# Cross-attention on one core: x's rows copied by ScalarE into two banks of PSUM, onto which the output's products are added, in place of GpSimd's additions

## The chip, the cores and the metric

The kernel runs on one core of a Trainium2 chip. The metric is the time of the program in microseconds of the device; the median of two runs of the kernel before is 1415.7 us (1415.37 and 1416.03). The engines are named as in the profile: PE is TensorE (matmuls), PEld its loading of weights, DVE is VectorE, ACT is ScalarE, POOL is GpSimd, SP is SyncE, which here issues nearly all transfers.

## The reference

For each of 64 images, x has 256 rows of 512 and the context 256 rows of 384, all in float32:

```python
text_p = einsum('bld,dh->blh', H_l, W_text) + b_text
audio_p = einsum('bsd,dh->bsh', H_a, W_audio) + b_audio
Q = layer_norm(text_p, g1, beta1)
K = layer_norm(audio_p, g2, beta2)
V = audio_p
scores = einsum('blh,bsh->bls', Q, K) * scale
alpha = softmax(scores)
H_hyper = einsum('bls,bsh->blh', alpha, V)
H_hyper = einsum('blh,hk->blk', H_hyper, W_out) + b_out
return layer_norm(H_hyper + H_l, g_out, beta_out)
```

H_l is x, and the last line adds x to the output's product before the last normalisation. That addition is what the change moves.

## The kernel before, in words

W_audio and W_out are folded once into one matrix wao of 384x512 with a bias bao (fold_multiply L248, fold_bias L263), so that an image's output is softmax times context, times wao, plus bao, plus x.

**Tiles.** An image is 256 rows, two tiles of 128 partitions. Each of the three large products of an image (q, k and y, class Blocks, L466) is made of seven products of blocks instead of eight: L487 multiplies sums of blocks of the left side by sums of blocks of the weights, and leave() (L491 to L515) adds the seven results into the quarters of the output with VectorE. GpSimd makes the sums of the left sides: sum_x (L310, xsum), sum_c (L326, csum for k, zsum for y). The seven results stand in four banks of PSUM, in pairs: (1,6), (2,5), (3,4) and (7). A bank holds 128x512 float32. leave(1) puts product 1 plus the bias into the upper half of the output's rows; leave(6), leave(2,5), leave(3,4) and leave(7) each add to what stands there, so they follow one another. Every bank read by leave is an addition of 128x512 on VectorE at L499.

**Banks.** PSUM has eight banks here. The pool p_pj (L81) has six, used in turn: a request takes the bank that was asked for six requests earlier and waits until that one's last reader is done. The pool p_at (L82) has two, for the scores (L526), the context products (ps_z, L592) and transposes.

**Order.** The schedule is written by hand: each engine carries out its instructions in the order in which the program names them, and waits on semaphores for what it needs of others. The main loop (L886) works on several images in one pass. With b as the pass: scores and softmax of image b (at); the q and k products of image b+2; the context and the y products of image b-1 (last); the rest of the output of image b-2 (done). A pass's order, as far as the change touches it:

- at.scores(), then done.o.leave(3,4), done.o.leave(7) and done.add_x(): the last two banks of y leave and GpSimd adds x's rows to y's rows (L608, two instructions of 128x512)
- turn_next: VectorE's transposes (L91) of x and the context of a later image, GpSimd's xsum and csum
- maxima and exponentials, q's first two products and leaves, division of e
- done.statistics(): ScalarE reads y's rows for mean and squares (L617, L622)
- q's other products and leaves, q's squares on ScalarE (L392) and their roots on GpSimd (L353, L355)
- q.turn (L91), done.shift (L729), last.context (the z products L592, zT copied by ScalarE L599), q.affine and k.affine (ScalarE L458), k.turn (L451), done.settle (L738), done.store
- q's normalise (ScalarE L420) and store
- last.start_products(): GpSimd makes zsum (L331 to L334)
- k's seven products and leaves, k's squares (L392), roots, normalise (L420) and store
- y's products: (1,6), their leaves, (2,5), their leave, (3,4), (7); the leaves of (3,4) and (7) fall in the next pass

Images 62 and 63 are worked off behind the loop with plain matmuls (L639, L692) and add x in another way (L648, L772), which the change leaves alone.

x's rows (x_rows) are loaded in a pass (L112, 512 KB) and, until now, first read two passes later, by add_x. The pool xin has three buffers.

Of the kernel before, what the change touches and what calls it, by code (L numbers as in the profile page):

```python
# [9 lines left out]
F32 = mybir.dt.float32  # L10
AF = mybir.ActivationFunctionType
ALU = mybir.AluOpType
AX = mybir.AxisListType
PSUM = bass.MemoryType.PSUM

P = 128
# [6 lines left out]
def kernel(  # L23
# [41 lines left out]
    nc = tc.nc  # L65
    ctx.enter_context(tc.manual_schedule())
    B, L, D = x.shape
    S, DA = c.shape[1:]
    H = w_text.shape[1]
    LT, ST = L // P, S // P  # L70
# [7 lines left out]
    work = ctx.enter_context(tc.tile_pool(name="work", bufs=2))  # L78
    small = ctx.enter_context(tc.tile_pool(name="small", bufs=4))
    scratch = ctx.enter_context(tc.tile_pool(name="scratch", bufs=3, space=bass.MemoryType.DRAM))  # L80
    p_pj = ctx.enter_context(tc.tile_pool(name="p_pj", bufs=6, space=PSUM))  # L81
    p_at = ctx.enter_context(tc.tile_pool(name="p_at", bufs=2, space=PSUM))  # L82

    def squares(dst, src):
# [11 lines left out]
    def load_c(b):  # L96
        cq = blk.tile([P, S // SQ, DA // NQ], F32, tag="cq", name=f"cq_{b}")
        squares(cq, c[b])
        blocks[b] = [cq]

    def load_x(b):
        xq = blk.tile([P, L // SQ, D // NQ], F32, tag="xq", name=f"xq_{b}")
        squares(xq, x[b])
        blocks[b].append(xq)
# [5 lines left out]
    def load_x_rows(b):  # L110
        x_rows[b] = xin.tile([P, LT, D], F32, tag="x", name=f"x_{b}")
        nc.sync.dma_start(x_rows[b], x[b].rearrange("(t p) d -> p t d", p=P))  # L112

    def load_c_rows(b):
        c_rows[b] = cin.tile([P, ST, DA], F32, tag="c", name=f"c_{b}")
        nc.sync.dma_start(c_rows[b], c[b].rearrange("(t p) d -> p t d", p=P))
# [16 lines left out]
    def row(v, name):  # L133
        t = const.tile([P, H], F32, tag=name, name=name)
        nc.sync.dma_start(t, v.rearrange("(o h) -> o h", o=1).broadcast_to([P, H]))
        return t
# [8 lines left out]
    x_rows, c_rows = {0: x_0}, {0: c_0}  # L145
# [54 lines left out]
    class RowTurn:  # L200


        def __init__(self, rows_sb, chunks, name):
            self.rows, self.chunks = rows_sb, chunks
            tag = "yr" if chunks == DC else "kT"
            self.ar = work.tile([P, 2, chunks, P], F32, tag=tag, name=f"{name}r")
            self.T = work.tile([P, chunks, 2 * P], F32, tag=name, name=f"{name}_0")
# [38 lines left out]
    ps_wao = {}  # L246

    def fold_multiply(a):  # L248

        ps = ps_wao[a] = p_pj.tile([P, D], F32, tag="pj", name="ps_wao")  # L250
        for k in range(HC):
            nc.tensor.matmul(  # L252
                ps,
                lhsT=waT[k][:, bass.ts(a, P)],
                rhs=wo_sb[:, k, :],
                start=(k == 0),
                stop=(k == HC - 1),
            )
# [32 lines left out]
    H2 = H // 2  # L291
# [34 lines left out]
    def sum_c(cT, tag="csum"):  # L326

        part = lambda i, j: cT[:, j, bass.ts(i, P)]
        s = work.tile([P, 5, P], F32, tag=tag, name=tag)
        add = nc.gpsimd.tensor_tensor  # L330
        add(s[:, 0], part(1, 0), part(1, 1), ALU.add)  # L331
        add(s[:, 1], s[:, 0], part(0, 0), ALU.subtract)
        add(s[:, 2:4], cT[:, 0:3:2, :P], cT[:, 0:3:2, P:], ALU.subtract)
        add(s[:, 4], part(0, 1), s[:, 1], ALU.subtract)  # L334
        return {
            1: [part(0, 0)], 2: [part(0, 1), part(0, 2)], 4: [part(1, 1), part(1, 2)],
            5: [s[:, 0], part(1, 2)], 6: [s[:, 1]], 7: [s[:, 2]], 3: [s[:, 4], s[:, 3]],
        }
# [127 lines left out]
    class Blocks(Projection):  # L466
# [7 lines left out]
        def __init__(self, name, b, sides, weights, bias):  # L474
            super().__init__(name, b, None, None, bias, None, 2)
            self.sides, self.weights, self.banks = sides, weights, {}

        def products(self, *ns):

            for n in ns:  # L480
                group = next(g for g in ((1, 6), (2, 5), (3, 4), (7,)) if n in g)
                if group not in self.banks:
                    self.banks[group] = p_pj.tile([P, 2, H2], F32, tag="pj", name=f"ps_{self.name}")
                place = self.banks[group][:, group.index(n), :]
                pairs = list(zip(self.sides[n], self.weights[n]))
                for i, (side, w) in enumerate(pairs):
                    nc.tensor.matmul(  # L487
                        place, lhsT=side, rhs=w, start=(i == 0), stop=(i == len(pairs) - 1)
                    )

        def leave(self, *ns):  # L491
# [22 lines left out]
    class Attention:  # L514
# [86 lines left out]
        def start_products(self):  # L601

            self.o = Blocks("y", self.b, sum_c(self.zT, "zsum"), wao_blocks, bao_sb)
            self.y = self.o.rows

        def add_x(self):
            for t in range(LT):
                nc.gpsimd.tensor_tensor(self.y[:, t, :], self.y[:, t, :], x_rows[self.b][:, t, :], ALU.add)  # L608

        def statistics(self, lo=0, n=LT):  # L610

# [151 lines left out]
    def turn_next(b):  # L763
        xT[b] = turn_x(b)
        xs[b] = sum_x(xT.pop(b))
        cT[b] = turn_c(b)
        cs[b] = sum_c(cT.pop(b))

    def add_bias(b):
        xb = x_rows[b]  # L770
        for t in range(LT):
            nc.gpsimd.tensor_tensor(xb[:, t, :], xb[:, t, :], bao_sb, ALU.add)  # L772

    assert B > 3
    q, k, xT, cT = {}, {}, {}, {}
# [66 lines left out]
    xs = {1: sum_x(xT[1])}  # L842
    k[1].scales()
    fold_multiply(0)
    fold_multiply(1)
    g1_sb, be1_sb, g2_sb, be2_sb, bac_sb = take_columns()

# [27 lines left out]
    cT[2] = turn_c(2)  # L875
    cs[2] = sum_c(cT[2])
    fold_multiply(2)
    fold_evict(2)
    bao_sb = fold_bias(part)
# [5 lines left out]
    done = last = None  # L885
    for b in range(B - 2):  # L886
        three = b + 3 < B
        at = Attention(b)
        at.scores()
        if done:  # L890
            done.o.leave(3, 4)
            done.o.leave(7)
            done.add_x()
        if three and b:
            turn_next(b + 3)
        if last:
            last.turn_e()
        at.maxima()
        at.exponentials()
        if not b:  # L900
            k[1].turn()
        q2 = q[b + 2] = Blocks("q", b + 2, xs.pop(b + 2), wt_blocks, bt_sb)
        q2.products(*((1, 6) if b else (1, 2, 6)))
        q2.leave(1)
        q2.leave(6)
        at.reciprocals()
        at.divide_e()
        if not b:
            k[1].affine(g2_sb, be2_sb)
        if b:  # L910
            q[b + 1].fetch()
            k[b + 1].fetch()
        at.store_e()
        if b + 4 < B:
            load_c(b + 4)
        if not b:
            at.fetch_e()
        if b + 4 < B:
            load_x(b + 4)
        if b:  # L920
            at.fetch_e()
            load_x_rows(b)
            load_c_rows(b)
        if not three:
            load_x_rows(b + 1)
            load_c_rows(b + 1)
        if b == 1:
            go_sb = row(g_out, "go")
            beo_sb = row(beta_out, "beo")
        if done:  # L930
            done.statistics()
        q2.products(*((2, 5) if b else (5,)))
        q2.leave(2, 5)
        q2.products(3, 4)
        q2.leave(3, 4)
        q2.products(7)
        q2.leave(7)
        q2.square()
        q2.scales()
        q[b + 1].turn()  # L940
        if not b:
            turn_next(3)
        if done:
            done.shift(0)
            done.shift(1)
        if last:
            last.context()
        q[b + 1].affine(g1_sb, be1_sb)
        if b:
            k[b + 1].turn()  # L950
            k[b + 1].affine(g2_sb, be2_sb)
        if done:
            done.settle(0)
            done.settle(1)
            done.store()
        q2.normalise()
        q2.store()
        if last:
            last.start_products()
        k2 = k[b + 2] = Blocks("k", b + 2, cs.pop(b + 2), wa_blocks, ba_sb)  # L960
        k2.products(1, 6)
        k2.leave(1)
        k2.leave(6)
        k2.products(2, 5)
        k2.leave(2, 5)
        k2.products(3, 4)
        k2.leave(3, 4)
        k2.products(7)
        k2.leave(7)
        k2.square()  # L970
        k2.scales()
        k2.normalise()
        k2.store()
        if last:
            last.o.products(1, 6)
            last.o.leave(1)
            last.o.leave(6)
            last.o.products(2, 5)
            last.o.leave(2, 5)
            last.o.products(3, 4)  # L980
            last.o.products(7)
        done, last = last, at
# [7 lines left out]
    at.scores(end=True)  # L990
    done.o.leave(3, 4)
    done.o.leave(7)
    done.add_x()
    add_bias(B - 2)
    last.turn_e()
    at.maxima()
# [19 lines left out]
    last.o.products(7, 3)  # L1016
    last.o.leave(3, 4)
    last.o.leave(7)
    last.add_x()
    at.context()  # L1020
    done.settle(1)
    done.store()
# [72 lines left out]
```

## Time and profile before

| what | value |
|---|---|
| median of two runs | 1415.7 us (1415.37 to 1416.03) |
| span of the profiled execution, first to last instruction | 1411.8 us |
| span below the median | 3.9 us |
| mean granted TensorE clock | 0.999 of full speed |
| main loop, one pass | 21.58 us |
| TensorE busy in one pass (721.44 to 743.02 us) | 21.58 us |
| VectorE, ScalarE, GpSimd busy in that pass | 19.09, 14.58, 13.52 us |
| DMA's share in that pass | 0.85 |

The profile gives for the profiled execution its span alone; the time of a run also holds what lies around the span.

The rows that belong to the change are GpSimd's additions of x at L608 (124 of 1277 ns, 155.7 us in all) and the groups of L499. A group's line gives line, engine, operation, tiles and shape, count, busy time, mean of one in ns, and then the engine's idle time just before these instructions and what ended most of it. An engine's idle time costs nothing by itself where the engine is not the one that sets the pace. TensorE's rows: a float32 matmul shows as two rows, and a row of 128x256 reads 379 ns although a new row begins every 0.216 us, since they overlap.

### The profile page before, as it was taken

How to read it: one execution, taken by the hardware profiler on the slowest of the kernel's cores; microseconds unless marked ns; L12 is line 12 of the kernel's file. 1: busy time of each engine (PE TensorE's matmuls, PEld its weight loads, DVE VectorE, ACT ScalarE, POOL GpSimd, SP SyncE). 2: the span in 40 equal slices, each digit the busy share in tenths (PEclk: the TensorE clock that was granted, in tenths of full speed). 3: DMA queues.
4: the chain of work that ended last, by engine and by line, in shares of the span. 5: the costliest groups of instructions: out<-in, count | busy, mean ns of one | idle time of the engine just before them, and what ended most of it. 6: DMA issues, size and time to landing. Idle time of an engine off the chain costs nothing.

```text
span 1411.8 us, 22761 instructions
## 1 busy us (share of the span) xinstructions
PE 1403.2 (99%) x6437; PEld 1220.4 (86%) x6437; DVE 1230.4 (87%) x1758; ACT 935.0 (66%) x2298; POOL 871.0 (62%) x1294
## 2 busy tenths in 40 slices
PE   9999999999999999999999999999999999999998
PEld 5888888888888888888888888888888888888885
DVE  6888898898888988988988889889889888898887
ACT  4667667676676676676766766766767667667663
POOL 5556666656656666666566566666665665666645
PEclk9999999999999999999999999999999999999999
DMA  8798877888888887787887887877888888878763
GB/s 211 206 259 229 245 233 218 246 232 224 241 243 219 232 233 228 234 226 237 231 230 235 225 238 232 231 232 232 221 243 237 222 240 239 222 235 232 223 212 125
DMA packets 450437, 322.32 MB, mean 228 GB/s; under 512 B 154885, under 2 KB 382981, under 8 KB 450310
## 3 DMA queue, kind: packets, MB, share of 16 engines
q1 hardware_dynamic: 450214, 320.72, 80.3%
q8 instruction: 52, 0.85, 0.3%
q14 instruction: 75, 0.61, 0.2%
q10 hardware_dynamic: 96, 0.13, 0.0%
HBM read 203.83 MB, written 116.92 MB: 227 GB/s over the span
## 4 chain that ended last, share of the span: by engine, by line
PE 98%; DVE 1%; POOL 1%; DMA 0%; ACT 0%; issue 0%; DVEq 0%; ACTq 0%
PE ps_q L487 27%; PE ps_k L487 21%; PE ps_y L487 20%; PE ps_sc L526 15%; PE ps_z L592 12%; PE ps_wao L252 1%; PE ps_y L639 1%; PE ps_q L374 0%; PE ps_k L374 0%; DMA c<-in_ctx_dram 0%; DVE yr L499 0%; PE ps_rows L214 0%; POOL yr L608 0%; POOL x L772 0%; DVE kr L499 0%; PE ps_wa L227 0%
## 5 line engine op out<-in xcount | busy, mean ns | idle before, releaser
L499 DVE TENSOR_TENSOR qr<-ps_q,qr 128x512 f32<-128x512 f32 x252 | 174.3, 692 | 88.9 <-PE ps_q L487 86.1
L526 PE MATMUL ps_sc<-kT,qT 128*128 128x256 f32 x1024 | 231.5, 379 | 0.0
L353 POOL TENSOR_SCALAR ve<-var 128x2 f32<-128x2 f32 x126 | 43.4, 344 | 290.0 <-ACT junk L392 289.8
L526 PEld LDWEIGHTS ps_sc<-kT,qT 128*128 128x128 f32 x1024 | 194.6, 190 | 26.9 <-issue 0.5
L543 ACT ACTIVATE e<-ps_sc,nmx 128x256 f32<-128x256 f32 x128 | 59.4, 468 | 230.3 <-DVE nmx L536 230.3
L608 POOL TENSOR_TENSOR yr<-yr,x 128x512 f32<-128x512 f32 x124 | 155.7, 1277 | 70.8 <-DVE yr L499 70.8
L499 DVE TENSOR_TENSOR kr<-ps_k,kr 128x512 f32<-128x512 f32 x252 | 174.4, 692 | 22.5 <-DVE kr L499 0.9
L487 PE MATMUL ps_q<-wtsum,xsum 128*128 128x256 f32 x756 | 193.7, 379 | 0.0
L499 DVE TENSOR_TENSOR yr<-ps_y,yr 128x512 f32<-128x512 f32 x248 | 171.6, 692 | 21.7 <-DVE yr L499 0.5
L487 PE MATMUL ps_k<-wa,cT 128*128 128x256 f32 x630 | 177.1, 379 | 0.0
L592 PE MATMUL ps_z<-eT,c 128*128 128x256 f32 x768 | 176.2, 379 | 0.0
L487 PE MATMUL ps_y<-wao,zT 128*128 128x256 f32 x620 | 174.1, 379 | 0.0
L355 POOL TENSOR_TENSOR rstd<-ve,nhalf 128x2 f32<-128x2 f32 x192 | 157.3, 819 | 16.0
L592 PEld LDWEIGHTS ps_z<-eT,c 128*128 128x128 f32 x768 | 145.9, 190 | 20.3 <-issue 0.5
L487 PEld LDWEIGHTS ps_q<-wtsum,xsum 128*128 128x128 f32 x756 | 143.6, 190 | 19.5
L458 ACT ACTIVATE qT<-qT,columns 128x256 f32<-128x256 f32 x256 | 133.0, 593 | 4.1 <-DVE qT L91 4.0
L458 ACT ACTIVATE kT<-kT,columns 128x256 f32<-128x256 f32 x256 | 132.2, 588 | 2.3 <-DVE kT L91 1.3
L487 PEld LDWEIGHTS ps_k<-wa,cT 128*128 128x128 f32 x630 | 119.6, 190 | 16.2
L487 PEld LDWEIGHTS ps_y<-wao,zT 128*128 128x128 f32 x620 | 117.7, 190 | 16.0
L420 ACT ACTIVATE kr<-kr,rstd 128x512 f32<-128x512 f32 x126 | 84.0, 714 | 71.6 <-POOL rstd L355 71.6
L392 ACT ACTIVATE junk<-kr 128x512 f32<-128x512 f32 x126 | 79.4, 630 | 77.9 <-DVE kr L499 73.5
L487 PE MATMUL ps_q<-wt,xT 128*128 128x256 f32 x504 | 129.0, 379 | 0.0
(160 smaller groups left out, 2976.3 us busy)
## 6 DMA issues: line engine op xcount, KB each, us to landing
kd<-kr SPq DMA_DIRECT2D x64, 512.0 KB, 3.1
kq<-kd SPq DMA_DIRECT2D x256, 128.0 KB, 3.4
qd<-qr SPq DMA_DIRECT2D x64, 512.0 KB, 4.8
qq<-qd SPq DMA_DIRECT2D x256, 128.0 KB, 3.3
xq<-in_x_dram SPq DMA_DIRECT2D x252, 128.0 KB, 3.0
x<-in_x_dram SPq DMA_DIRECT2D x63, 512.0 KB, 4.3
out_dram<-yr SPq DMA_DIRECT2D x62, 512.0 KB, 4.8
cq<-in_ctx_dram SPq DMA_DIRECT2D x252, 96.0 KB, 2.5
```

Source lines behind the costliest of these rows:

```text
L252: nc.tensor.matmul(ps, lhsT=waT[k][:, bass.ts(a, P)], rhs=wo_sb[:, k, :], start=(k == 0), stop=(k == HC - 1),)
L353: nc.gpsimd.tensor_scalar(ve, var, EPS, None, ALU.add)
L355: nc.gpsimd.tensor_tensor(r, ve, nhalf[:, :n], ALU.pow)
L392: nc.scalar.activation(junk, self.rows[:, t, :], AF.Square, scale=1.0 / math.sqrt(H), accum_out=self.var[:, t : t + 1],)
L420: nc.scalar.mul(row, row, self.r[t])
L458: nc.scalar.activation(self.T[:, k, :], self.T[:, k, :], AF.Identity, bias=bet[:, k : k + 1], scale=gam[:, k : k + 1],)
L487: nc.tensor.matmul(place, lhsT=side, rhs=w, start=(i == 0), stop=(i == len(pairs) - 1))
L499: add = lambda o, i0, i1: nc.vector.tensor_tensor(o, i0, i1, ALU.add)
L526: nc.tensor.matmul(self.sc[:, t, :], lhsT=self.qT[:, k, bass.ts(t, P)], rhs=self.kT[:, k, :], start=(k == 0), stop=(k == HC - 1),)
L543: nc.scalar.activation(self.e[:, t, :], self.sc[:, t, :], AF.Exp, bias=self.nmx[:, t : t + 1], accum_out=self.den[:, t : t + 1],)
L592: nc.tensor.matmul(ps[:, j, :], lhsT=c_rows[self.b][:, s, bass.ts(lo + j, P)], rhs=self.eT[:, s, :], start=(s == 0), stop=(s == ST - 1),)
L608: nc.gpsimd.tensor_tensor(self.y[:, t, :], self.y[:, t, :], x_rows[self.b][:, t, :], ALU.add)
```

## The change

p_pj gets four banks instead of six, and a new pool p_sd gets the other two. y's blocks are seeded: in start_products, behind zsum, GpSimd subtracts one quarter of x's rows from another in place (128x256), and ScalarE copies two pairs of quarters (128x512 each) into the two banks of p_sd. The products (2,5) and (3,4) of y are then added onto these banks: their first matmul has start=False. The two matmul groups that make the first two parts of wao use the same two banks at the head. add_x and its three calls go. The in-place subtraction makes up for leave(3,4), which builds the first quarter of the output from the third, where x's third quarter then already is. The order of all other instructions on every engine stays: TensorE, VectorE and SyncE have the same instructions in the same order, ScalarE has 124 copies more, GpSimd 124 additions less and 62 subtractions more.

```diff
-    p_pj = ctx.enter_context(tc.tile_pool(name="p_pj", bufs=6, space=PSUM))
+    p_pj = ctx.enter_context(tc.tile_pool(name="p_pj", bufs=4, space=PSUM))
+    p_sd = ctx.enter_context(tc.tile_pool(name="p_sd", bufs=2, space=PSUM))
...
     def fold_multiply(a):
-        ps = ps_wao[a] = p_pj.tile([P, D], F32, tag="pj", name="ps_wao")
+        pool, tag = (p_sd, "sd") if a < 2 else (p_pj, "pj")
+        ps = ps_wao[a] = pool.tile([P, D], F32, tag=tag, name="ps_wao")
...
             self.sides, self.weights, self.banks = sides, weights, {}
+            self.seeded = ()
+
+        def seed(self, rows):
+
+            self.seeded = ((2, 5), (3, 4))
+            quarters = rows.rearrange("p t (k h) -> p (t k) h", k=2)
+            nc.gpsimd.tensor_tensor(quarters[:, 0], quarters[:, 0], quarters[:, 2], ALU.subtract)
+            for group, some in zip(self.seeded, (quarters[:, 1:3], quarters[:, 0:4:3])):
+                self.banks[group] = p_sd.tile([P, 2, H2], F32, tag="sd", name="ps_sd")
+                nc.scalar.copy(self.banks[group], some)
...
                     nc.tensor.matmul(
-                        place, lhsT=side, rhs=w, start=(i == 0), stop=(i == len(pairs) - 1)
+                        place,
+                        lhsT=side,
+                        rhs=w,
+                        start=(i == 0 and group not in self.seeded),
+                        stop=(i == len(pairs) - 1),
+                        skip_group_check=group in self.seeded,
                     )
...
             self.o = Blocks("y", self.b, sum_c(self.zT, "zsum"), wao_blocks, bao_sb)
+            self.o.seed(x_rows[self.b])
             self.y = self.o.rows
-
-        def add_x(self):
-            for t in range(LT):
-                nc.gpsimd.tensor_tensor(self.y[:, t, :], self.y[:, t, :], x_rows[self.b][:, t, :], ALU.add)
...
             done.o.leave(7)
-            done.add_x()
```

The same call of add_x goes at two places behind the loop.

More of the change, by code (lines that the diff above doesn't have):

```diff
@@ L992 @@
     done.o.leave(7)
-    done.add_x()
     add_bias(B - 2)
@@ L1018 @@
     last.o.leave(7)
-    last.add_x()
     at.context()
```

## The prediction

> **What bounds the kernel now.** I read the page first, for the engine without idle time; then the chain that ended last, to see whether the same engine carries it; then the timeline of one steady pass of the main loop, engine by engine, since the change moves work between engines that the average calls free.
>
> ```profile
> span 1411.8 us, 22761 instructions
> PE 1403.2 (99%) x6437; PEld 1220.4 (86%) x6437; DVE 1230.4 (87%) x1758; ACT 935.0 (66%) x2298; POOL 871.0 (62%) x1294
> PE 98%; DVE 1%; POOL 1%; DMA 0%; ACT 0%; issue 0%; DVEq 0%; ACTq 0%
> ```
>
> TensorE is busy for 99% of the span and makes 98% of the chain. The lists of waits put nothing in front of a matmul but a few tenths of a microsecond at the head and the tail. So GpSimd's 62% and ScalarE's 66% are no limit by themselves: no work taken from them can shorten the loop. Only a new wait in front of TensorE can change the time much, and the search is for one.
>
> VectorE, TensorE, ScalarE and GpSimd in the same pass (columns: start us, us from first to last, engine, line, tiles, idle before and its releaser):
>
> ```profile
> 714.30 0.69 DVE L499 TENSOR_TENSOR qr<-ps_q,qr 128x512 f32<-128x512 f32 x1 [0.17 <-PE ps_q L487]
> 714.91 1.23 DVE L91 STREAM_TRANSPOSE qT<-qq 128x1024 f32<-128x1024 f32 x1
> 716.07 1.37 DVE L729 SCALAR_TENSOR_TENSOR yr<-yr,nm,go 128x512 f32<-128x512 f32 x2
> 717.36 1.29 DVE L451 STREAM_TRANSPOSE kT<-kq 128x512 f32<-128x512 f32 x2
> 718.58 2.07 DVE L738 SCALAR_TENSOR_TENSOR yr<-yr,rstd,beo 128x512 f32<-128x512 f32 x2
> 720.57 0.68 DVE L499 TENSOR_TENSOR kr<-ps_k,ba 128x512 f32<-128x512 f32 x1
> 721.28 3.08 DVE L499 TENSOR_TENSOR kr<-ps_k,kr 128x512 f32<-128x512 f32 x4
> ```
> ```profile
> 721.00 0.59 PE L487 MATMUL ps_k<-wasum,csum 128*128 128x256 f32 x2
> 721.44 0.59 PE L487 MATMUL ps_y<-wao,zT 128*128 128x256 f32 x2
> 722.30 1.03 PE L487 MATMUL ps_y<-wao,zT 128*128 128x256 f32 x4
> ```
> ```profile
> 716.18 0.56 ACT L599 COPY zT<-ps_z 128x512 f32<-128x512 f32 x1
> 721.11 1.32 ACT L420 ACTIVATE qr<-qr,rstd 128x512 f32<-128x512 f32 x2
> 723.60 0.63 ACT L392 ACTIVATE junk<-kr 128x512 f32<-128x512 f32 x1 [1.17 <-DVE kr L499]
> ```
> ```profile
> 718.92 1.17 POOL L333 TENSOR_TENSOR zsum<-zT 128x256 f32<-128x256 f32 x1
> 720.05 0.91 POOL L334 TENSOR_TENSOR zsum<-zT,zsum 128x128 f32<-128x128 f32 x1
> 727.36 2.50 POOL L608 TENSOR_TENSOR yr<-yr,x 128x512 f32<-128x512 f32 x2 [1.15 <-DVE yr L499]
> ```
>
> The reader is to see a lag. TensorE has finished k's products and starts y's at 721.44 (a matmul is two rows, one row every 0.2159 us; a pass is 100 rows, 21.585 us). VectorE at that moment has only just begun to take k's banks out: leave(1) at 720.57, leave(6) from 721.28 to 721.97 (0.69 for one), then (2,5), (3,4), (7) every 0.80 us. It was held from 714.30 by the last q bank, which only TensorE's own order releases, and ran from there without idle time. TensorE does not notice, since six banks let it run ahead.
>
> **The change, part by part.** *Removed:* 124 additions on GpSimd, 1277 ns each (155.7 us on the page), two per pass. They lie beside TensorE's scores, and xsum, which follows them, is wanted a pass later. Worth nothing to the loop.
>
> *Six banks become four.* Each pass asked the pool p_pj for 12 banks in turn: q's four, k's four, y's four. Request n takes the bank of request n-6, so y's (1,6) took q's (3,4), which VectorE had left at 714.13. Now a pass asks for 10 (y's (2,5) and (3,4) come from p_sd) and request n takes the bank of n-4: y's (1,6) takes k's (1,6). The order of instructions in the changed kernel shows the same: the first matmul of y waits for VectorE's leave(6) of this pass's k. That ends at 721.974 and TensorE wants the bank at 721.437: 0.537 late. Set beside the times of this trace, every other bank that the loop asks for is free in time. This one is late by 0.53 to 0.54 us in each of 58 passes, and by 1.27, 1.37 and 0.15 in the first three.
>
> *What a wait costs beyond its lateness.* One such wait stands in the trace, at the tail:
>
> ```profile
> 1382.09 0.45 POOL L332 TENSOR_TENSOR zsum<-zsum,zT 128x128 f32<-128x128 f32 x1
> 1382.59 0.73 PEld L487 LDWEIGHTS ps_y<-waosum,zsum 128*128 128x128 f32 x4 [0.51 <-POOL zsum L332]
> ```
>
> GpSimd ends at 1382.54, the weight load starts at 1382.59, and the second matmul row stands 0.32 behind the first in place of 0.216: 0.05 + 0.11 = 0.16 us. So the wait is 0.537 + 0.16 = 0.70 us per pass.
>
> *Does it come back each pass?* Yes: VectorE's next q bank waits for TensorE, so a later TensorE moves the whole stretch 714.30 to 721.97. The loop is then y, scores and q on TensorE (66 rows, 14.25 us, and 0.20 to VectorE's start), 7.67 us on VectorE from the last q bank to the end of k's leave(6), and 0.16: 22.28 us against 21.585, again 0.70.
>
> *Added on ScalarE:* two copies of 128x512 per pass behind the normalising of q, which ends at 722.43 (instructions overlap by 0.09, so the first copy starts at 722.34). Nearest rows: the copy out of PSUM, 0.56, and the slowest 128x512 row on this engine that carries no bias, 0.71. I take 0.57, since it is the same operation. The first copy ends at 722.91; with 0.16 y's (2,5) can start at 723.07. Behind the late (1,6) products it would want to start at 721.974 + 0.16 + 4 x 0.216 = 723.00. So the seed adds 0.07 (0.21 at 0.71; 0 if the copy takes under 0.50). The second copy has 1.7 us more. Behind the copies stand the squares of k, which today wait 1.17 us until 723.60; both copies end by then, at 723.4 to 723.7. The copies' own waits are for x's rows (loaded a pass earlier) and for banks that VectorE left some 16 us before.
>
> *Added on GpSimd:* one subtraction 128x256 behind zsum, 0.73 (xsum's row) to 1.17 (L333 beside VectorE). It ends by 722.1 and is wanted by the second copy, at 722.9: hidden. If that slack were gone, y's (3,4) still has until 724.6.
>
> *SyncE's queue* is unchanged, instruction for instruction, and so is the number of matmuls; a matmul that adds to its bank shows the same 379 ns row as one that does not.
>
> *Head and tail.* At the head the third product of W_out takes the bank of q's (1,6) of image 1: wanted at 38.57, left at 40.90, so 2.33 + 0.16 = 2.5 us once. The first three passes then add 0 (VectorE's backlog there is worked off behind the same delay) to 2.4; I take 1. At the tail the additions were in front of zsum, where TensorE lost some 0.1 us: nothing.
>
> **Sum:** 58 x 0.77 + 2.5 + 1 = 48 us on a span of 1411.8. The span is 3.9 below the median 1415.7, which I take as lying around it both times: 1415.7 + 48 = 1464.
>
> **Two gates, nearly tied.** Without any lateness of leave(6), y's (2,5) would start at 722.30, as now; the first copy lets it start at 723.07 at the earliest. ScalarE alone therefore costs 0.77 us per pass: its work from the division of e at 711.50 to 722.43 runs without a pause of note, and it too starts behind a q bank that only TensorE frees. The two waits overlap, and are not to be added up: the later one counts, 0.77.
>
> [...] The settling rows of VectorE (L738, median 1104 ns in the loop, 744 on the last image's rows) are slow beside zsum, not beside the removed additions, while a leave beside those additions keeps its 692. By the rows the instruction that slows VectorE stays, and nothing is won. [...] For the copy the row out of PSUM is 0.56. [...]
>
> **Rivals.** (1) *The lag is used up once, no real change.* TensorE waits at the first y, and from there on runs later against VectorE and ScalarE, which keep their places and finish in time. Price: 0.77 + 3.5, 1420. It decides if neither engine waits for TensorE's q: VectorE's idle time there would have to be nothing. For it: the 1.27, 1.37 and 0.15 of the first passes, where VectorE works off a backlog. Against it: in the pass shown VectorE idles 0.32, 0.24, 1.04 and 0.17 us for q's banks, 1.77 in all, so it follows TensorE. (2) *ScalarE becomes the bound alone.* A write to PSUM is not in the trace. If it went at the pace of the SBUF row L458 (593 ns for 256 columns, so 1.18 for 512), y's (2,5) would start at 723.68 and not 722.30: 1.38 per pass, 80 + 3.5, 1499. Against it: the copies of 512 out of PSUM at 0.56 to 0.57. (3) *The subtraction meets VectorE.* At 1.17 in place of 0.73 beside k's leaves it could push them by up to 0.2 each pass, 0.90 in all: 52 + 3.5, 1471. Against it: the 692 of a leave beside L608. (4) *VectorE's stretch gets shorter.* If settling ran at 0.745, 2.07 would become 1.41 and leave(6) would be in time; the copy would hold the 0.77, and the time stays 1464. It is no way back by itself.
>
> **How the numbers follow.** Forecast, with (4): 0.80; rival (1) 0.06; (2) 0.07; (3) 0.06; something faster 0.01. Low end: the lateness alone, 58 x 0.537 = 31, 1446. High end: 58 x (0.70 + 0.21 + 0.2) + 5 = 69, 1485. The measurement tells about 2%, 28 us, from no change: slower than 1444 is the forecast with (2) and (3), 0.92 with a hundredth left out for a partial wait; within 2%, 0.07.
>
> **What would show it.** Right: TensorE idle about 0.75 us once per pass in front of ps_y<-wao,zT, most of it released by VectorE's kr at leave(6), the rest by ScalarE's first copy, busy share near 96%, a pass of about 22.35 us; VectorE's idle time in front of q's banks grown by the same; ScalarE's copies near 0.57. Wrong: no idle time there (rival 1), or idle time of over 1 us in front of the (2,5) products released by ScalarE (2), or settling or k's leaves longer than now (3).

## The result, and the profile after

The changed kernel takes 1472.15 us (median of two runs, 1471.81 to 1472.5) against 1415.7: a ratio of 1.040, with a 95% interval of 1.038 to 1.042. It is slower by 56.5 us. The profiled execution has a span of 1470.0 us against 1411.8, 58.2 more. In every run that lists both, the time lies 1.7 to 1.9 us above the span (1471.81 above 1470.0 here), so the span of 1411.8 belongs to an execution of about 1413.6 us, 2 us quicker than the median; that is why the spans differ by more than the medians.

The page of the changed kernel, its first lines and the engines' shares of the chain:

```profile
span 1470.0 us, 22586 instructions
PE 1422.3 (97%) x6437; PEld 1211.5 (82%) x6437; DVE 1230.6 (84%) x1758; ACT 996.7 (68%) x2422; POOL 761.6 (52%) x1232
PE 46%; DVE 29%; DMA 11%; issue 7%; ACT 4%; SPq 3%; POOL 0%; DVEq 0%; ACTq 0%
```

GpSimd has lost 109 us of work and ScalarE has gained 62, as the change intends. Yet the span grew. TensorE carries out the same 6437 rows, but where it made 98% of the chain it now makes 46%: the chain leaves TensorE wherever TensorE waits. It passes through VectorE, and from there on to ScalarE and to transfers. The transfers do not set the pace: between 80 and 1430 us the lists of waits of TensorE, VectorE, ScalarE and GpSimd name no transfer.

A steady pass of the changed kernel, each engine around the start of y (columns as in the prediction):

```profile
727.25 0.68 DVE L516 TENSOR_TENSOR kr<-ps_k,ba 128x512 f32<-128x512 f32 x1
727.96 3.08 DVE L516 TENSOR_TENSOR kr<-ps_k,kr 128x512 f32<-128x512 f32 x4
728.77 0.30 PEld L499 LDWEIGHTS ps_y<-wao,zT 128*128 128x128 f32 x2 [0.89 <-ACT qr L422]
728.80 0.67 PE L499 MATMUL ps_y<-wao,zT 128*128 128x256 f32 x2 [0.52 <-DVE kr L516]
729.02 1.09 ACT L488 COPY ps_sd<-x 128x512 f32<-128x512 f32 x2
729.64 0.73 PEld L499 LDWEIGHTS ps_sd<-wao,zT 128*128 128x128 f32 x4
729.74 1.04 PE L499 MATMUL ps_sd<-wao,zT 128*128 128x256 f32 x4
730.28 0.63 ACT L394 ACTIVATE junk<-kr 128x512 f32<-128x512 f32 x1 [0.17 <-DVE kr L516]
```

leave(6) is the first of the four rows from 727.96 and ends at 728.66. The weight load of y's first matmul starts 0.11 us later. ScalarE's first copy ends at 729.59 and the weight load of y's (2,5) starts 0.05 us later. Both waits that the prediction names are there, one after the other, and with either of them gone the other would still hold TensorE for nearly as long. The weight load's bracket names ScalarE's L422, the normalising of q. That is a slip of the inference: the matmul's own bracket names VectorE's kr, and in the first experiment below the wait goes when leave(6) comes earlier, with the normalising where it was.

The lists of waits for TensorE and its weight loads show that it comes back in each pass (columns: total us, times, longest):

```profile
PE ps_y L499 <- DVE kr L516: 31.4, 61, 0.5
PE ps_sd L499 <- ACT ps_sd L488: 4.8, 2, 3.4
PE ps_wao L254 <- DVE qr L516: 3.0, 1, 3.0
```
```profile
PEld ps_y L499 <- ACT qr L422: 53.5, 60, 0.9
PEld ps_sd L499 <- ACT ps_sd L488: 6.4, 5, 3.8
```

The first list counts time with no matmul row open, and a row reads 379 ns though rows follow every 216, so it understates the loss; the starts of the rows are the better measure. Set row by row against the kernel before (the two have the same rows in the same order), TensorE in the profiled execution falls behind as follows:

| where | lost, us | forecast |
|---|---|---|
| head, at the third product of W_out | 4.79 | 2.5 |
| first pass that has a y | 2.03 | 1 for the first three passes |
| the other 60 passes, 0.766 each | 45.97 | 0.77 each |
| last y, behind the loop | 5.38 | 0 |
| sum | 58.17 | 48 |

A pass takes 22.35 us (starts of y, 22.34 to 22.36) against 21.583.

The head, TensorE's granted clock by stretch (columns: stretch, its length, busy us and rows of each engine, then PEclk, DMA's share, GB/s), and the first rows behind the wait:

```profile
38.40:41.60 3.20, 0.20 (x2) 0.04 (x1) 2.57 (x4) 2.33 (x5) 0.00 (x0) 1.00 1.01 301
41.60:45.90 4.30, 4.30 (x6) 1.79 (x7) 4.03 (x5) 2.10 (x6) 1.14 (x3) 0.60 0.91 238
45.90:47.70 1.80, 1.80 (x6) 0.81 (x5) 0.00 (x0) 0.71 (x2) 1.72 (x3) 1.00 1.20 224
```
```profile
41.59 5.37 PE L254 MATMUL ps_wao<-wo,waT 128*128 128x512 f32 x8 [3.00 <-DVE qr L516]
```

The wait itself is 3.0 us, against the 2.5 that was priced. Behind it the clock falls to 0.60 in the mean: four rows begin 0.85 us apart in place of 0.43, and that is the other 1.7 us.

The tail, in order of time:

```profile
1434.17 0.59 PE L499 MATMUL ps_sd<-wao,zT 128*128 128x256 f32 x2
1436.82 0.72 POOL L485 TENSOR_TENSOR x<-x 128x256 f32<-128x256 f32 x1
1437.57 0.59 ACT L488 COPY ps_sd<-x 128x512 f32<-128x512 f32 x1 [3.99 <-POOL x L485]
1438.21 0.95 PE L499 MATMUL ps_sd<-waosum,zT 128*128 128x256 f32 x2 [3.44 <-ACT ps_sd L488]
1438.96 1.06 PE L499 MATMUL ps_sd<-wao,zT 128*128 128x256 f32 x2
```

There the products are called in the order 1, 2, 4, 6, 5, and 4 lies in the bank of (3,4). Its copy waits for GpSimd's subtraction, which stands behind all of zsum. So TensorE waits 3.6 us by the starts of its rows for the second copy, and then again runs on a lower clock: rows 0.427 apart in place of 0.216, at a granted clock of 0.58 from 1438.20 to 1440.20 us and 0.62 from there to 1442.50.

### The profile page after: what moved, and what is told of

The parts are those of the page before. It is cut to its first block, busy times and chain, and to the rows that moved or that the text cites. A ratio compares the mean times of both kernels' runs of the same rounds, so it can differ in the third digit from the quotient of the medians.

```text
span 1470.0 us, 22586 instructions
## 1 busy us (share of the span) xinstructions
PE 1422.3 (97%) x6437; PEld 1211.5 (82%) x6437; DVE 1230.6 (84%) x1758; ACT 996.7 (68%) x2422; POOL 761.6 (52%) x1232
## 4 chain that ended last, share of the span: by engine, by line
PE 46%; DVE 29%; DMA 11%; issue 7%; ACT 4%; SPq 3%; POOL 0%; DVEq 0%; ACTq 0%
PE ps_sc L543 15%; PE ps_sd L499 15%; PE ps_q L499 9%; DMA cq<-in_ctx_dram 8%; DVE yr L752 8%; PE ps_y L499 6%; DVE kr L516 6%; DVE qr L516 5%; DVE kT L453 5%; ACT e L574 3%; DVE yr L743 3%; SPq L578 1%; SPq L89 1%; DVE qT L92 1%; PE ps_y L653 1%
## 5 line engine op out<-in xcount | busy, mean ns | idle before, releaser
L318 POOL TENSOR_TENSOR xsum<-xT 128x256 f32<-128x256 f32 x63 | 45.9, 729 | 198.5 <-DVE xT L92 198.5
L499 PE MATMUL ps_sd<-wao,zT 128*128 128x256 f32 x496 | 138.8, 382 | 1.4 <-ACT ps_sd L488 1.3
L422 ACT ACTIVATE kr<-kr,rstd 128x512 f32<-128x512 f32 x126 | 84.0, 714 | 72.2 <-POOL rstd L357 72.2
L752 DVE SCALAR_TENSOR_TENSOR yr<-yr,rstd,beo 128x512 f32<-128x512 f32 x124 | 127.4, 1065 | 0.6 <-POOL rstd L357 0.6
L574 ACT ACTIVATE e<-e,rden 128x256 f32<-128x256 f32 x124 | 56.2, 500 | 83.9 <-DVE rden L570 83.9
L499 PE MATMUL ps_k<-wasum,csum 128*128 128x256 f32 x378 | 112.4, 379 | 0.0
```

The costliest lines, as they stand in the source:

```text
L422: nc.scalar.mul(row, row, self.r[t])
L499: nc.tensor.matmul(place, lhsT=side, rhs=w, start=(i == 0 and group not in self.seeded), stop=(i == len(pairs) - 1), skip_group_check=grou ...
L574: nc.scalar.mul(self.e[:, t, :], self.e[:, t, :], self.rden[:, t : t + 1])
L752: nc.vector.scalar_tensor_tensor(self.y[:, t, :], self.y[:, t, :], self.r[t], beo_sb, ALU.mult, ALU.add)
```

## The experiments

The theory: two waits, for the bank (leave(6) of k) and for ScalarE's first copy, overlap almost exactly; either alone costs a pass some 0.7 us, so that taking away one wins nothing or little, and taking away both wins all. The rivals: the bank alone, or the copies alone.

**The bank's wait taken away.** VectorE's settling goes behind leave(6):

```diff
-        if done:
-            done.settle(0)
-            done.settle(1)
-            done.store()
         q2.normalise()
...
         k2.leave(6)
+        if done:
+            done.settle(0)
+            done.settle(1)
+            done.store()
         k2.products(2, 5)
```

> The changed kernel with VectorE's two settling instructions (and the store behind them) put behind leave(6) of k instead of ahead of leave(1), so that leave(6) ends some 2 us before TensorE asks for its bank. Theory (two waits that overlap, the bank and ScalarE's first copy, the later one counts): the pass stays at 22.35 us, because the copy still holds y's (2,5); TensorE's idle time moves from y's (1,6) to y's (2,5), about 0.77 us once a pass; time 1470 to 1473. Rival (the bank alone costs the time): the pass falls to 21.58 us and the time by 46 us, to 1426.

Measured: 1473.96 us, ratio 1.041 (1.040 to 1.043). A pass is 22.35 us. The place of the wait moved, as the timeline of this kernel shows:

```profile
752.51 0.41 PEld L499 LDWEIGHTS ps_y<-wao,zT 128*128 128x128 f32 x2
752.72 0.59 PE L499 MATMUL ps_y<-wao,zT 128*128 128x256 f32 x2
753.62 1.09 ACT L488 COPY ps_sd<-x 128x512 f32<-128x512 f32 x2
754.24 0.73 PEld L499 LDWEIGHTS ps_sd<-wao,zT 128*128 128x128 f32 x4 [0.90 <-ACT ps_sd L488]
```

y's (1,6) start without a wait, though ScalarE is at its normalising of q beside them (752.39 to 753.71), and (2,5) stand still until the copy is done. The bank alone is not the cause: without its wait nothing is won. The time is 1 us above the range expected; in this execution TensorE loses 7.1 us at the head, against 4.8 in the changed kernel's.

**The copies' wait taken away.** The subtraction and the copies move to the start of the pass, where ScalarE is idle:

```diff
             done.o.leave(7)
+        if last:
+            last.seed()
...
             self.o = Blocks("y", self.b, sum_c(self.zT, "zsum"), wao_blocks, bao_sb)
-            self.o.seed(x_rows[self.b])
+            self.o.seeded = tuple(self.sd)
+            self.o.banks.update(self.sd)
```

seed() now belongs to Attention and keeps the two banks in self.sd; behind the loop it is called at the same place.

> The changed kernel with GpSimd's subtraction and ScalarE's two copies moved to the start of the pass, behind the leaves of (3,4) and (7) of the image before, where ScalarE waits for the scores' maxima. Theory: the wait for leave(6) of k is left, 0.68 us a pass as the changed kernel's trace shows it in front of y's (1,6); the pass is 22.27 us; the tail's 5.4 us and 1.5 us of the first pass go as well: 1472 - 60 x 0.08 - 7 = 1460. Rival (ScalarE's copies alone cost the time): the pass falls to 21.58 us and the time to 1421.

Measured: 1464.84 us, ratio 1.035 (1.033 to 1.036). A pass is 22.340 us, 0.757 more than before the change and not 0.68: I had read the shift at the first row of y alone, and the second row adds 0.076 (in the changed kernel it begins 0.291 us behind the first, at 728.800 and 729.091, in place of 0.216). The tail's loss is gone, and the first pass's has shrunk from 2.03 to 0.35 us (TensorE is 51.0 us behind at the end, of it 5.6 up to and with the first y). In each pass the wait for leave(6) is left, with no copy in front of y:

```profile
PE ps_y L490 <- DVE kr L507: 31.1, 60, 0.5
```

**Both taken away.** The two edits together.

> Both edits together: settling behind leave(6), and the seeds at the start of the pass. Theory: no wait is left in the loop, the pass is 21.58 us as before the change; the head's 4.8 us stay: 1420 to 1421. Rival (seeding or four banks cost something besides these two waits): the pass stays above 21.7 us, the time above 1428.

Measured: 1419.68 us, ratio 1.0029 (1.0019 to 1.0040). A pass is 21.583 us again, and TensorE is 4.1 us behind from the first y to the end. The time is slightly below the range expected, since the head costs 3.6 us in this execution and not 4.8. TensorE's share is back:

```profile
PE 1403.7 (99%) x6437; PEld 1220.5 (86%) x6437; DVE 1183.8 (84%) x1758; ACT 996.5 (70%) x2422; POOL 708.0 (50%) x1232
```

So seeding, four banks, and the matmuls that add onto a bank cost nothing in the loop by themselves; what is left lies at the head.

**The banks alone.** The pools as in the change, but nothing is copied or subtracted, and GpSimd adds x as in the kernel before:

```diff
-            self.o.seed(x_rows[self.b])
+            for group in ((2, 5), (3, 4)):
+                self.o.banks[group] = p_sd.tile([P, 2, H2], F32, tag="sd", name="ps_sd")
...
             done.o.leave(7)
+            done.add_x()
```

> The division of the banks alone: p_pj with four, the (2,5) and (3,4) products of y in the two of p_sd, but nothing copied or subtracted, and x added by GpSimd as in the kernel before. Theory: the wait for leave(6) alone, 0.68 us a pass (22.27), and the head's 4.8 us; the GpSimd additions cost nothing: 1415.7 + 61 x 0.68 + 4.8 = 1462. Rival (the copies alone cost the time): 1421.

Measured: 1465.08 us, ratio 1.035 (1.033 to 1.036), and a pass of 22.34 us, as with the seeds moved. As there, the 0.68 us of the expectation is 0.757. The bank's wait is shown by itself:

```profile
PE ps_y L499 <- DVE kr L516: 31.4, 61, 0.5
```

The two kernels differ in the 155.7 us of GpSimd's additions and in 67.5 us of ScalarE's copies, and are equal in time: the additions that the change removes were worth nothing.

**The copies swapped.** The bank of (3,4) is filled first, that of (2,5) second:

```diff
-            for group, some in zip(self.seeded, (quarters[:, 1:3], quarters[:, 0:4:3])):
+            for group, some in zip(self.seeded[::-1], (quarters[:, 0:4:3], quarters[:, 1:3])):
```

> The changed kernel with the order of ScalarE's two copies swapped: the bank of (3,4) is filled first, that of (2,5) second, while TensorE still wants (2,5) first. Theory (the first wanted copy is the later of two nearly tied waits): y's (2,5) starts one copy's step later, 0.515 us in the changed kernel's trace, so the pass is 22.86 us and the time 1472 + 61 x 0.515 = 1503. Rival (the bank wait covers the copies, which have slack): 22.35 us and 1472, as without the swap.

Measured: 1505.78 us, ratio 1.064 (1.062 to 1.065). A pass is 22.86 us, the 0.51 us of one copy's step above the changed kernel. The copies have no slack: their order alone is worth 34 us. The few microseconds above the 1503 lie at the head (6.3 us lost there in this execution) and in the tail.

**Both, and the head.** As with both edits, and the third product of W_out takes a bank of p_at:

```diff
-        pool, tag = (p_sd, "sd") if a < 2 else (p_pj, "pj")
+        pool, tag = (p_sd, "sd") if a < 2 else (p_at, "at")
```

> Settling behind leave(6), the seeds at the start of the pass, and the third product of W_out at the head in a bank of p_at, so that it no longer waits for a bank that VectorE leaves at the end of image 1's q. Theory: the head's wait of 3 us and the 1.7 us of halved TensorE clock behind it go, and nothing is left: 1415.5, within 1 us of the kernel before. Rival (the head's loss has another cause, or the matmuls there run slowly whatever waits): 1419 to 1420 as without this edit.

Measured: 1416.4 us, ratio 1.0011 (1.0002 to 1.0020). The head's loss falls from 3.6 to 1.0 us in the traces; 2.0 us come back at the first y, where no settling was there to be moved and k's leaves are late by VectorE's backlog. The time is 0.9 us above the 1415.5 that was expected. This is the best version with the seeds, and it does not beat the kernel before: in the loop TensorE is without idle time in both.

## Why the prediction was right

**The bound and the gate.** TensorE sets the pace, and a new wait in front of it is what counts. Right: the removed 155.7 us are worth nothing (banks alone against seeds moved, 1465.08 and 1464.84).

**The bank's lag.** 0.537 us of lateness, read from the trace of before, plus the restart, which is what a wait costs beyond its lateness. Right in place and lateness; the restart was priced at 0.16 and measured at 0.22 (0.757 a pass). The one row that it was taken from is a wait for GpSimd, where the weight load starts 0.05 us behind the end; behind VectorE's leave it starts 0.11 behind.

**ScalarE's copy.** 0.57 us taken, 0.577 measured; 0.77 us a pass, 0.766 measured. Right. With the larger restart the bank's 0.757 is only 0.01 less. The two are nearer to a tie than the prediction had them: it put the bank 0.07 below the copy. A pass came out as forecast because the copy, which was priced well, is the later of the two.

**Coming back each pass.** Right: 61 waits. The prediction's loop, 14.25 + 0.20 + 7.67, comes with a restart of 0.22 to 22.34 us, which is the pass of the two kernels that keep the bank's wait alone. One sign that it named is weak: VectorE's idle time in front of q's banks was to grow by the same 0.75 a pass, and it grew from 105.5 us in the list of waits to 140.9, some 0.58 a pass. With both edits, where the wait is gone, it is 143.8, since VectorE's settling is shorter there (745 ns against 1061 before); so this row does not tell the wait from its absence. Rival (1), a lag used up once, falls. Rival (2) falls by the copy's 0.577, rival (3) by the subtraction's 0.725 and k's leaves at an unchanged 0.692. What (4) said, that freeing VectorE alone wins nothing, is what the first experiment shows.

**Head and tail.** Here the sum was short by 10 us, the whole difference between 48 and 58 (8 us against the medians, 1464 and 1472.15). Three terms were mis-sized. The head's 2.5 is 4.79: the wait was there, 3.0 us long, but the slow clock behind it was missing. The first three passes' 1 is 3.6 (2.03 and twice 0.77): they lose as the others do, and the first more, since ScalarE's copy comes late there. And the tail's "nothing" is 5.38: the step looked at GpSimd's additions alone and did not walk the order of the products there, where the second copy is wanted third. Two readings were loose without changing the sum: the 3.9 us that the prediction took as lying around the span is 1.8, and its lists of waits also hold 1.5 us in front of the very first matmul, which the changed kernel has too.

**The settling's pace.** The prediction kept the settling at its slow row, because zsum stays beside it. In the changed kernel it is so, 1065 ns for settling and 1169 for zsum's longest instruction:

```profile
L752 DVE SCALAR_TENSOR_TENSOR yr<-yr,rstd,beo 128x512 f32<-128x512 f32 x124 | 127.4, 1065 | 0.6 <-POOL rstd L357 0.6
L335 POOL TENSOR_TENSOR zsum<-zT 128x256 f32<-128x256 f32 x62 | 72.5, 1169 | 0.0
```

With both edits, where settling has next to no work of GpSimd beside it:

```profile
L753 DVE SCALAR_TENSOR_TENSOR yr<-yr,rstd,beo 128x512 f32<-128x512 f32 x124 | 87.6, 745 | 0.6 <-POOL rstd L357 0.6
L335 POOL TENSOR_TENSOR zsum<-zT 128x256 f32<-128x256 f32 x62 | 45.7, 738 | 0.0
```

Beside each other, settling and zsum's longest instruction take 1065 and 1169 ns; apart, 745 and 738. Why the pair is slow, no run shows. In these runs the time of settling went with the GpSimd instruction beside it, not with how much GpSimd does: it took 1061 ns in the kernel before, with 109 us more work on GpSimd. In the first experiment, where settling stands beside the subtraction, it takes 974 and the subtraction 1165 in place of 725. For ScalarE's copy the prediction went by the row out of PSUM, and that was near enough: the copy of 128x512 from x's rows into a bank of p_sd takes 577 ns, that out of PSUM into zT 564.

## What to carry to other kernels

Where one engine is without idle time, price a change by the waits that it puts in front of that engine, not by the work that it takes from others (here 0.77 us a pass lost, against 155.7 us of additions that were worth nothing): fewer banks mean that a request meets a younger reader (with four banks in place of six, y's first met a leave that ended 0.537 us late), and the lag of that reader can be read from the trace of before. Look for a second wait just behind the first, since two that nearly tie hide each other, and removing one shows little (1473.96 and 1464.84 us with one gone and 1419.68 with both gone, against 1472.15). Walk the head and the tail by their own order, as a step that is hidden in the loop need not be hidden there (the second copy, 3.6 us at the tail).

## What the runs showed of the hardware that was not expected

Behind a wait of some 3 us TensorE's clock can be lower, and need not be. At the head of the changed kernel, after 3.0 us, rows of 512 columns begin 0.85 us apart in place of 0.43, with a granted clock of 0.60 in the mean over 4.3 us; the first two rows behind the wait still run at nearly full pace, and the drop comes about 1 us later. In the tail, after 3.6 us, rows of 256 begin 0.427 apart in place of 0.216, from the second row on. At the head a drop followed the wait of 3.5 us with the seeds moved, that of 3.9 us with the settling moved, and the one with the copies swapped too. But behind two of nearly the same length there was none, that of both edits and that of the banks alone:

```profile
PE ps_wao L254 <- DVE qr L507: 3.3, 1, 3.3
PE ps_wao L254 <- DVE qr L516: 3.1, 1, 3.1
```

The idle time of the weight loads of these products tells the two kinds apart (the changed kernel, seeds moved, copies swapped, settling moved; then both edits, banks alone):

```profile
PEld ps_wao L254 <- issue: 9.3, 21, 3.4
PEld ps_wao L254 <- issue: 9.8, 21, 3.9
PEld ps_wao L254 <- issue: 9.8, 21, 4.1
PEld ps_wao L254 <- issue: 10.6, 21, 4.2
PEld ps_wao L254 <- issue: 8.4, 21, 3.6
PEld ps_wao L254 <- issue: 8.3, 21, 3.5
```

Without the longest, the other twenty come to 5.7 to 6.4 us in the first four and to 4.8 in the last two. That is 0.24 each, as in the kernel before, where the rows begin 0.43 apart throughout. So between 3.0 and 3.3 us the length of the wait alone does not decide, and what does was not tried. Part of the changed kernel's loss at the head, 1.7 of 4.79 us, may thus differ from one execution to the next. The waits of 0.77 us in every pass leave the clock at full (1.00 from 80 to 1430 us).

A wait of TensorE costs more than its lateness: 0.16 us behind GpSimd's zsum (one wait, in the kernel before) and 0.22 behind VectorE's leave(6): 0.11 from the leave's end to the weight load, and 0.11 from this load, which begins with no matmul row open, to the next (728.77 and 728.88). Behind ScalarE's copy the weight load starts 0.05 us after the end, as behind GpSimd. Why the end of VectorE's leave takes 0.06 us longer to reach TensorE was not tried.
